# A pre-activation block with look-up convolutions: its products in four column tiles of 128 rows and 32 columns

## The chip, the cores and the metric

The kernel runs on one core of one Trainium2 chip. A core has five engines with a queue each: TensorE (PE in the profile, its weight loads PEld), VectorE (DVE), ScalarE (ACT), GpSimd (POOL) and SyncE (SP, which here only issues DMAs). TensorE writes to PSUM, which VectorE and ScalarE read. The metric is the device time of one execution in microseconds; lower is better. The kernel before took 2607.75 us in the median of three runs (2605.92 to 2608.51).

## The reference

The input is 16 images of 256 channels with 28 x 28 points, fp32. It is normalised over groups of 8 channels, passed through two "look-up" convolutions with batch norm between and after them, gated by a squeeze-and-excite layer, and added to the input.

```python
def amm_conv3x3(x, centroids, w_sub):              # centroids (256, 16, 9), w_sub (256, 9, 256)
    p = the 3x3 patches of each channel            # (b, n, c, 9), n = 28*28
    d = sum(p*p) - 2*einsum('bncs,cks->bnck', p, centroids) + sum(centroids*centroids)
    attn = softmax(-d, axis=-1)                    # over 16 centroids
    lut = einsum('cks,cso->cko', centroids, w_sub)
    return einsum('bnck,cko->bno', attn, lut)

x0 = groupnorm(x)
out = relu(bn1(amm_conv3x3(x0, centroids1, wsub1)))
out = bn2(amm_conv3x3(out, centroids2, wsub2))
out = out * sigmoid(relu(mean(out) @ w1 + b1) @ w2 + b2)
result = x + relu(out + x0)
```

So for each channel and point there is a softmax over 16 distances, the mean of the 16 centroids under it (9 numbers), and then a product of these 256 x 9 numbers with `w_sub` to 256 output channels. That last product is the one the change touches.

## The kernel before

**Blocks.** The work of a layer and an image is cut in four blocks: half of the input channels (`hh`, 128 of them) times half of the rows (`t`, 14 rows of 28 points, N = 392 columns). 2 layers x 16 images x 4 make 128 blocks. For each of them TensorE runs:

- `logits` (line 613, tile name `lg`): four calls of 16 matmuls with 32 rows and 32 columns of weights, one for each of the 16 places (4 row groups, 4 column groups) of the array. ScalarE turns the result into exponentials `e` (line 624).
- `num_b` (line 678, `nb`): the denominators and the ninth of the weighted means, 32 matmuls of 64 rows and 32 columns that accumulate over four steps.
- `num_a` (line 664, `na`): the other eight means, four calls of eight matmuls of 64 rows and 32 columns.

VectorE takes the reciprocals and spreads them over partitions, VectorE and GpSimd scale the means, and nine operands `q` of 128 x 392 are ready for each block (tiles `qp`, two in each, and `qo`).

**Products.** `product` (lines 744 to 751, tile `acc`) multiplies nine `q` by nine weight matrices of 128 x 128 and accumulates in one PSUM bank. The 2 x 2 blocks of channels and rows are combined with sums of weights and differences of `q` (made by `mix` on GpSimd, line 757), so that seven products are enough where eight would be needed; one of the seven is issued in two parts, of seven matmuls and of two. That is eight calls of `product` for each layer and image, listed in `PRODUCTS` (lines 45 to 48). ScalarE (line 779) and VectorE (lines 785 and 787) take the results out of PSUM. The very last product is cut in two halves of 196 columns.

**Small matmuls.** Beside products stand `gn_mean` and `gn_var` (lines 534 and 551, `gnp`: group means and variances of the next image, 128 x 128 weights `gmat`, 2 to 4 columns), `center_add` (line 343, `sqp`), `rest_sum` (line 1146, once at the end), `se_hidden` (line 1041, `sep`: 128 rows, 32 columns of weights, 1 column of data) and `se_gate` (line 1049, 32 rows and 128 columns).

**Order.** The order of every engine's queue is written by hand. `at(cl, sub, f, ...)` files a call under a step and a place within it, and in the end all calls are issued in the order of these keys; each engine then works through its own in that order, and semaphores hold an instruction back until its operands are there. Between two products stand calls of `lg`, `na` or `nb`, so that TensorE changes between forms of tiles all the time. PSUM is used as four pairs of banks, handed out by the tables `ROLES` and `EARLY`.

**How fp32 shows.** Each fp32 matmul of the program stands in the trace as two weight loads and two matmuls ("passes"), so a product of nine is 18 rows of LDWEIGHTS and 18 of MATMUL.

Of the kernel before, what the change touches and what calls it, by code (L numbers as in the profile page):

```python
# [17 lines left out]
P = 128  # L18
# [59 lines left out]


BIAS_ROW = 11  # L80


def rows_of(m, c, a):
# [5 lines left out]
def kernel(  # L89
# [22 lines left out]
    nc = tc.nc  # L112
# [9 lines left out]
    one = const.tile([P, 1], F32, name="one")  # L122
# [3 lines left out]
    gmat = const.tile([P, P], F32, name="gmat")  # L126
# [18 lines left out]
    def bank(name, step=None, role=None, tag=None):  # L145
        return banks(name, step, role, tag)[:, 0, :]
# [4 lines left out]
    def view(t, off, dims):  # L151
        return bass.AP(t.tensor, t.offset + off, [list(d) for d in dims])
# [25 lines left out]
    def spare_of(n0, n, i=0):  # L178
        return pts[i].rearrange("p s n -> p (s n)")[:, n0 : n0 + n]
# [14 lines left out]
    def load(ap, name, eng=None):  # L194
        t = const.tile(list(ap.shape), ap.dtype, name=name)
        (eng or nc.sync).dma_start(t, ap)
        return t
# [18 lines left out]
    wl = {n: walls[i // 3][:, i % 3] for i, n in enumerate(("S1", "S2", "S4", "A12", "S3", "A22"))}  # L216
# [37 lines left out]
    first = io.tile([P, 1568], F32, tag="pb", name="first")  # L254
# [25 lines left out]
    nhalf_sb = load(nhalf, "nhalf_sb")  # L280
# [28 lines left out]
    def rsqrt(dst, src, eps, n):  # L309
        t = small.tile([P, n], F32, name="rs_t")  # L310
        nc.gpsimd.tensor_scalar(t, src, eps, None, op0=ALU.add)
        nc.gpsimd.tensor_tensor(dst, t, mhalf[:, :n], ALU.pow)
# [20 lines left out]
    def small_bank(name, step, tag=None):  # L333
        return bank(name, step, step and ROLES["small"][step % 2], EARLY["small"].get(step) if tag is None else tag)
# [5 lines left out]

    def center_add(wf, c0, w, sq, step=None):
        ps = small_bank("sqp", step)
        nc.tensor.matmul(ps[:, :w], lhsT=nhalf_sb, rhs=sq[:, :w], start=True, stop=True)  # L343
        nc.vector.tensor_add(wf[:, c0 : c0 + w], wf[:, c0 : c0 + w], ps[:, :w])

    def center_sum(wf, n):
# [162 lines left out]
    def border(u, p):  # L509
# [18 lines left out]
        ends = row[:, :, 0 : W : W - 1]  # L528
        eng.tensor_tensor(ends, ends, view(tm, 16 * (4 + 2 * t) + 8 * p, [tm.ap[0], [1, 8], [16, 2]]), ALU.add)

    def gn_mean(b, k0=0, n=NB, step=None):
        st, mv = gst[b]
        ps = small_bank("gnp", step)[:, : 2 * n]
        nc.tensor.matmul(  # L534
            ps, lhsT=gmat, rhs=mv[:, k0 : k0 + n].rearrange("p b t -> p (b t)"), start=True, stop=True
        )
        gm = small.tile([P, NB, 2], F32, name="gn_gm")
        nc.vector.tensor_copy(gm[:, :n].rearrange("p b t -> p (b t)"), ps)
        dv = small.tile([P, NB], F32, name="gn_dv")
        nc.vector.tensor_sub(dv[:, :n], ps.rearrange("p (b t) -> p b t", t=2)[:, :, 0], mv[:, k0 : k0 + n, 0])  # L540
        for i in range(n):
            nc.vector.scalar_tensor_tensor(
                dv[:, i : i + 1], ps[:, 2 * i : 2 * i + 1], mv[:, k0 + i, 0:1], dv[:, i : i + 1],
                op0=ALU.subtract, op1=ALU.mult,
            )
        gst[b, "m"] = gm, dv

    def gn_var(b, k0=0, n=NB, step=None):
        gm, dv = gst.pop((b, "m"))
        ps = small_bank("gnp", step)[:, :n]  # L550
        nc.tensor.matmul(ps, lhsT=gmat, rhs=dv[:, :n], start=True, stop=True)  # L551
        var = small.tile([P, NB], F32, name="gn_var")
        rstd, shift = (nrm[:, b, i, k0 : k0 + n] for i in (1, 2))
        if n == 1:
            neg = small.tile([P, NB], F32, name="gn_neg")
            nc.vector.tensor_scalar_mul(neg[:, :n], gm[:, :n, 0], -1.0)
            nc.vector.scalar_tensor_tensor(var[:, :n], ps, GN_EPS, gm[:, :n, 1], op0=ALU.add, op1=ALU.add)
            nc.gpsimd.tensor_tensor(rstd, var[:, :n], mhalf[:, :n], ALU.pow)
            nc.gpsimd.tensor_tensor(shift, neg[:, :n], rstd, ALU.mult)
        else:  # L560
            nc.vector.tensor_add(var[:, :n], gm[:, :n, 1], ps)
            rsqrt(rstd, var[:, :n], GN_EPS, n)
            nc.gpsimd.tensor_tensor(shift, gm[:, :n, 0], rstd, ALU.mult)
            nc.gpsimd.tensor_scalar(shift, shift, -1.0, None, op0=ALU.mult)
# [177 lines left out]
    accs = {}  # L742

    def product(key, us, w, ks, first=True, last=True, step=None, cols=(0, N), tag=None):
        if first and key not in accs:
            accs[key] = bank("acc", step, step and ROLES["acc"][step % 2], EARLY["acc"].get(step) if tag is None else tag)
        for n, k in enumerate(ks):
            nc.tensor.matmul(  # L748
                accs[key][:, : cols[1] - cols[0]], lhsT=wl[w][:, k, :], rhs=us["q", k][:, cols[0] : cols[1]],
                start=first and n == 0, stop=last and n == len(ks) - 1,  # L750
            )

    def mix(out_u, mm, in0, in1):
        if mm == 4:
# [356 lines left out]
    vsum = spare_of(NB * S * P + 2 * N, NB * P, 1).rearrange("p (o n) -> p o n", o=NB)  # L1111
# [31 lines left out]
    def rest_sum(b, tag):  # L1143
        ps = bank("pv", tag=tag)[:, :NB]
        for o in range(NB):
            nc.tensor.matmul(ps[:, o : o + 1], lhsT=vsum[:, o, :], rhs=one, start=True, stop=True)
        ys[b, "rest"] = rest[:, 1]
        nc.vector.tensor_tensor(rest[:, 1], ps, rest[:, 0], ALU.mult)

# [86 lines left out]
    for j, u in enumerate(blocks):  # L1236
        gi, g = 8 * (j // 4), 2 * j
        for mm in range(5):
            kind = "one" if mm == 4 else "pair"
            t = g + 1 + (j > 2) if mm == 4 else g + 2 + (j > 1)  # L1240
# [59 lines left out]
    for l in range(2):  # L1300
        for b in range(B):
            n = l * B + b
            g = 8 * n
            us = blocks[4 * n : 4 * n + 4]
            for c, w, r, ks in PRODUCTS:
                if g + c == 5:
                    for sub, k0, k1 in ((0.8, 0, 5), (0.82, 5, 7), (0.84, 7, 9)):
                        at(4, sub, product, (n, c), us[r], w, ks[k0:k1], k0 == 0, k1 == 9, step=4)
                elif n == 2 * B - 1 and c == 11:
                    for sub, k0, k1 in ((1.95, 0, 5), (1.97, 5, 7), (1.99, 7, 9)):  # L1310
                        at(g + c, sub, product, (n, c), us[r], w, ks[k0:k1], k0 == 0, k1 == 9, tag=0)
                elif n == 2 * B - 1 and c in (9, 10):
                    at(g + c, 2.0, product, (n, c), us[r], w, ks, tag=c - 9)
                elif n == 2 * B - 1 and c == 12:
                    at(g + c, 1.99, open_last, n)
                    for h in range(2):
                        at(g + c, 2.0 + 0.02 * h, product, (n, 12 + h), us[r], w, ks, cols=(N // 2 * h, N // 2 * h + N // 2))
                else:
                    at(g + c, 1.32 if g + c == 7 else 2.0, product, (n, c), us[r], w, ks, step=g + c)
# [15 lines left out]
            if n == 2 * B - 1:  # L1335
# [13 lines left out]
                at(g + 11, 1.9, norm_out, l, b, *c12)  # L1349
                at(g + 11, 1.91, norm_out, l, b, *c22)  # L1350
                at(g + 11, 1.96, rest_sum, b, 1)
                at(g + 11, 1.98, se_hidden, b, None, 1)
                at(g + 11, 1.995, se_gate, b, None, 1)
# [23 lines left out]
            if l == 0:  # L1377
# [8 lines left out]
                if b + 1 < B:  # L1386
                    at(*(((8, 1.6) if b == 1 else (g - 2, 2.6)) if b else (1, 1.6)), load_x, b + 1)
                    for q in range(NB):
                        at(*(((g + 1, 1.5) if b == 1 else (g, 0.3)) if b else (4, 0.14)), gn_stats, b + 1, q)
                    at(*((g + 1, 2.1) if b else (4, 0.825)), gn_mean, b + 1, step=g + 1 if b else 4)  # L1390
                    at(*((g + 3, 2.1) if b else (4, 0.845)), gn_var, b + 1, step=g + 3 if b else 4)
                    for q in range(NB):
                        at(*((g + 4, 1.9) if b else (4, (0.95, 1.055)[q])), gn_apply, b + 1, q)
                        at(*((g + 4, 1.92) if b else (4 + 4 * q, 1.6 - 0.05 * q)), to_home1, b + 1, q)
            else:
                last = b == B - 1
# [93 lines left out]
    ps = bank("gnq", tag=3)  # L1490
# [59 lines left out]
    with tc.If(rv > 0):  # L1550
        with tc.For_i(0, B, 1) as it:
            t = io.tile([P, NB, HW], F32, tag="xt", name="xt")
# [6 lines left out]
            for k in range(NB):  # L1559
                gn_stats(B, k)  # L1560
            gn_mean(B)
            gn_var(B)
            for k in range(NB):
                gn_apply(B, k)
                nc.gpsimd.dma_start(home1[B][k * P : (k + 1) * P], twice(xpads[k]))
            for l in range(2):
# [6 lines left out]
                for t2 in range(2):  # L1573
                    us = []
# [51 lines left out]
def _lay_out(inputs):  # L1626
# [52 lines left out]
    for p in range(P):  # L1679
# [3 lines left out]
        for b in range(2):  # L1683
            before[p, b, : b * P + p] = 1.0
        nhalf[p, p - p % 16 + BIAS_ROW] = -0.5 if p % 16 in rows else 0.0
        if p % 16 == BIAS_ROW:
            a = (p // 16) % 2
# [37 lines left out]
```

## Time and profile before

| | |
|---|---|
| time, median of three runs | 2607.75 us (2605.92 to 2608.51) |
| the profiled execution, first to last instruction | 2606.2 us |
| TensorE busy, matmuls | 2591.2 us, 99%, 37026 instructions |
| TensorE busy, weight loads | 1273.2 us, 49% |
| VectorE, ScalarE, GpSimd busy | 1776.6, 1371.7, 1905.6 us |
| products, line 748, all groups, busy | 1097.5 + 182.4 + 157.9 us and a small group |
| `lg`, `na`, `nb`, busy | 469.0, 376.5, 375.2 us |

The profile is of one execution. Its span is what lies between its first and its last instruction; the timed runs include a little around it. A group of instructions is given as "line, engine, operation, out<-in, rows*columns of the weights, partitions x elements of the data, count". Busy time of a group is the time in which at least one of its instructions ran, while "mean ns" is the length of a single one; where matmuls overlap, as in a pipeline or in several tiles, the mean is longer than busy time over count. So 15872 `lg` passes of 499 ns are busy for only 469.0 us.

In the timeline, instructions of one kind that follow each other are merged in one row: its start, the time to the end of the last, and the count.

### The profile page before, as it was taken

Reading aid. Unit: us, or ns where it says so; the run is one execution under the profiler, and the core shown is the slowest. Engines: PE = TensorE matmul, PEld = TensorE weight load, DVE = VectorE, ACT = ScalarE, POOL = GpSimd, SP = SyncE. Lnnn points to the kernel's source line nnn. Section 1 sums busy time; section 2 is a strip of 40 time slices with the busy share of each in tenths; the row PEclk is TensorE's granted clock in tenths of the full one; section 3 lists DMA queues with packets and bytes.
Section 4 is the critical chain, followed back from the end, with each engine's and each line's share of the span. In section 5 each row is a group of like instructions: output and inputs, shape, how many; then the busy total and the mean of one; then the engine's idle time right before and its main releaser. Section 6 shows DMA issues by size and latency. Waiting matters only on the chain.

```text
span 2606.2 us, 85832 instructions
## 1 busy us (share of the span) xinstructions
PE 2591.2 (99%) x37026; PEld 1273.2 (49%) x37026; DVE 1776.6 (68%) x3797; ACT 1371.7 (53%) x1913; POOL 1905.6 (73%) x1341
## 2 busy tenths in 40 slices
PE   8999999999999999999999999999999999999999
PEld 4444455444454444544444444444444444444445
DVE  8766656666657666566676767766776667767676
ACT  6444444444444445444445555555555655555565
POOL 6687666776567776667666887878878787787786
PEclk9999999999999999999999999999999999999999
DMA  7556656565545575564664444444344444444442
GB/s 228 166 131 184 195 166 187 160 168 170 163 141 147 157 194 173 165 172 134 176 169 103 109 112 127 119 119 120 101 126 128 118 116 112 115 124 128 117 104 66
DMA packets 213288, 372.07 MB, mean 143 GB/s; under 512 B 29496, under 2 KB 183528, under 8 KB 212328
## 3 DMA queue, kind: packets, MB, share of 16 engines
q1 hardware_dynamic: 206584, 333.75, 47.6%
q0 software_dynamic: 6176, 32.66, 3.5%
q8 instruction: 295, 4.83, 0.8%
q14 instruction: 89, 0.73, 0.1%
q10 hardware_dynamic: 144, 0.10, 0.0%
HBM read 288.46 MB, written 77.95 MB: 141 GB/s over the span
## 4 chain that ended last, share of the span: by engine, by line
PE 99%; ACT 0%; POOL 0%; DVE 0%; issue 0%; DMA 0%; POOLq 0%; ACTq 0%
PE acc L748 52%; PE lg L613 17%; PE na L664 14%; PE nb L678 14%; ACT e L624 0%; PE sep L1049 0%; POOL qp L757 0%; PE sep L1041 0%; DMA xt<-in_x 0%; PE tap L392 0%; PE sqp L374 0%; PE sqp L343 0%; POOL qp L729 0%; PE gnp L534 0%; PE gnp L551 0%
## 5 line engine op out<-in xcount | busy, mean ns | idle before, releaser
L748 PE MATMUL acc<-qp,wall 128*128 128x392 f32 (+1 forms) x3088 | 1097.5, 498 | 0.3 <-POOL qp L757 0.2
L624 ACT ACTIVATE e<-lg 128x784 f32<-128x784 f32 x960 | 737.8, 820 | 635.2 <-PE lg L613 632.0
L757 POOL TENSOR_TENSOR qp<-qp,qp 128x784 f32<-128x784 f32 x512 | 943.7, 1867 | 152.0 <-DVE qp L740 151.6
L748 PEld LDWEIGHTS acc<-qp,wall 128*128 128x128 f32 x3088 | 567.4, 190 | 504.8 <-issue 53.6
L721 DVE STREAM_SHUFFLE rb<-r 128x392 f32<-128x392 f32 x1024 | 551.5, 606 | 0.0
L613 PE MATMUL lg<-pt,wd 32*32 32x392 f32 x15872 | 469.0, 499 | 0.2
L692 DVE SCALAR_TENSOR_TENSOR r<-nb,kst,r 128x392 f32<-128x392 f32 x128 | 80.1, 626 | 447.6 <-ACT r L688 447.6
L664 PE MATMUL na<-e,cwa 64*32 64x392 f32 x8192 | 376.5, 493 | 0.0
L740 DVE TENSOR_TENSOR qp<-na,rb 128x784 f32<-128x784 f32 x352 | 334.0, 972 | 62.2 <-PE na L664 50.3
L678 PE MATMUL nb<-e,cwb 64*32 64x392 f32 x8192 | 375.2, 492 | 0.1
L729 POOL TENSOR_TENSOR qo<-qo,rb 128x392 f32<-128x392 f32 x128 | 132.5, 1035 | 297.0 <-DVE rb L717 296.2
L706 DVE RECIPROCAL r<-r 128x392 f32<-128x392 f32 x128 | 333.2, 2603 | 4.4
L729 POOL TENSOR_TENSOR qp<-qp,rb 128x784 f32<-128x784 f32 x160 | 295.7, 1858 | 2.9
L678 PEld LDWEIGHTS nb<-e,cwb 64*32 64x32 f32 x8192 | 191.5, 106 | 174.7 <-issue 24.5
L664 PEld LDWEIGHTS na<-e,cwa 64*32 64x32 f32 x8192 | 183.8, 106 | 184.0 <-issue 74.8
L613 PEld LDWEIGHTS lg<-pt,wd 32*32 32x32 f32 x15872 | 116.4, 103 | 266.6 <-issue 238.3
L748 PE MATMUL acc<-qp,w_A 128*128 128x392 f32 x512 | 182.4, 499 | 0.0
L688 ACT ACTIVATE r<-nb,kst 128x392 f32<-128x392 f32 x128 | 86.7, 678 | 165.5 <-PE nb L678 162.3
L648 POOL TENSOR_TENSOR z<-z,mx 128x1568 f32<-128x1568 f32 x32 | 91.8, 2869 | 94.8 <-DVE mx L642 94.8
L748 PE MATMUL acc<-qo,wall 128*128 128x392 f32 (+1 forms) x386 | 157.9, 491 | 0.0
L734 ACT COPY qp<-na 128x784 f32<-128x784 f32 x160 | 130.0, 813 | 23.6 <-PE na L664 22.1
L748 PEld LDWEIGHTS acc<-qp,w_A 128*128 128x128 f32 x512 | 94.6, 190 | 82.5 <-DVE qp L740 19.8
(241 smaller groups left out, 1706.4 us busy)
## 6 DMA issues: line engine op xcount, KB each, us to landing
pt<-home SPq DMA_DIRECT2D x744, 209.0 KB
pt<-home SPq DMA_DIRECT2D x744, 104.5 KB
home<-xpad SPq DMA_DIRECT2D x30, 899.0 KB
xt<-in_x SPq DMA_DIRECT2D x30, 784.0 KB
out_dram<-y SPq DMA_DIRECT2D x31, 392.0 KB
pt<-in_p SPq DMA_DIRECT2D x6, 784.0 KB
d_wS<-st SPq DMA_DIRECT2D x12, 192.0 KB
wall<-d_wS SPq DMA_DIRECT2D x4, 576.0 KB
```

The lines of the kernel that those rows point to most:

```text
L613: nc.tensor.matmul(bk[32 * c : 32 * c + 32, :N].rearrange("p (r w) -> p r w", w=W), lhsT=(wx[u["hh"]] if early(u) else wts["wd", u["hh"]]) ...
L624: nc.scalar.activation(eg[:, 2 * i : 2 * i + 2, :], bk[:, :, :N], AF.Exp, scale=2.0)
L648: nc.gpsimd.tensor_tensor(zk, zk, mx.unsqueeze(2).to_broadcast([P, N // 4, K]), ALU.subtract)
L664: nc.tensor.matmul(bs[32 * i : 32 * i + 32, r, :N], lhsT=wts["cwa", u["hh"]][64 * r : 64 * r + 64, mm, i, :], rhs=es[64 * r : 64 * r + 64, ...
L678: nc.tensor.matmul(bs[32 * i : 32 * i + 32, r, :N], lhsT=wts["cwb", u["hh"]][64 * r : 64 * r + 64, mm, i, :], rhs=es[64 * r : 64 * r + 64, ...
L706: nc.vector.reciprocal(u["r"], u["r"])
L721: nc.vector.stream_shuffle(rb[:, r, :], u["r"], mask_of(2 * mm + r))
L729: nc.gpsimd.tensor_tensor(q, q, u.pop(("rb", mm)), ALU.mult)
L734: nc.scalar.copy(pair(u, mm), u.pop(("na", mm))[:, :, :N])
L740: nc.vector.tensor_mul(pair(u, mm), u.pop(("na", mm))[:, :, :N], rb)
L748: nc.tensor.matmul(accs[key][:, : cols[1] - cols[0]], lhsT=wl[w][:, k, :], rhs=us["q", k][:, cols[0] : cols[1]], start=first and n == 0, s ...
L757: nc.gpsimd.tensor_tensor(pair(out_u, mm), pair(in0, mm), pair(in1, mm), ALU.subtract)
```

## The change

`product` issues four matmuls for each of its nine operands in place of one. Each takes 32 of the 128 columns of the weights (`wl[w][:, k, o:o+32]`), all 128 rows and the same 392 columns of `q`, and writes 32 of the 128 partitions of the same PSUM bank. `start` and `stop` are set for each of the four as before. A helper `by_cols` does the same for the small matmuls of `center_add`, `gn_mean`, `gn_var` and `rest_sum`; `se_hidden` and `se_gate` are as they were. Nothing else differs: other engines have the same instructions in the same order, and lines after 548 move down by some (`product`'s matmul from 748 to 752, `lg` from 613 to 616, `na` from 664 to 667, `nb` from 678 to 681, `sep` from 1041 to 1045 and from 1049 to 1053; `gnp` is issued in `by_cols` at line 534).

```diff
+AW = 32
...
     def center_add(wf, c0, w, sq, step=None):
         ps = small_bank("sqp", step)
-        nc.tensor.matmul(ps[:, :w], lhsT=nhalf_sb, rhs=sq[:, :w], start=True, stop=True)
+        by_cols(ps[:, :w], nhalf_sb, sq[:, :w])
...
+    def by_cols(ps, lhsT, rhs):
+        for o in range(0, P, AW):
+            nc.tensor.matmul(ps[o : o + AW], lhsT=lhsT[:, o : o + AW], rhs=rhs, start=True, stop=True)
+
     def gn_mean(b, k0=0, n=NB, step=None):
...
-        nc.tensor.matmul(
-            ps, lhsT=gmat, rhs=mv[:, k0 : k0 + n].rearrange("p b t -> p (b t)"), start=True, stop=True
-        )
+        by_cols(ps, gmat, mv[:, k0 : k0 + n].rearrange("p b t -> p (b t)"))
...
     def gn_var(b, k0=0, n=NB, step=None):
...
-        nc.tensor.matmul(ps, lhsT=gmat, rhs=dv[:, :n], start=True, stop=True)
+        by_cols(ps, gmat, dv[:, :n])
...
         for n, k in enumerate(ks):
-            nc.tensor.matmul(
-                accs[key][:, : cols[1] - cols[0]], lhsT=wl[w][:, k, :], rhs=us["q", k][:, cols[0] : cols[1]],
-                start=first and n == 0, stop=last and n == len(ks) - 1,
-            )
+            for o in range(0, P, AW):
+                nc.tensor.matmul(
+                    accs[key][o : o + AW, : cols[1] - cols[0]], lhsT=wl[w][:, k, o : o + AW],
+                    rhs=us["q", k][:, cols[0] : cols[1]], start=first and n == 0, stop=last and n == len(ks) - 1,
+                )
...
     def rest_sum(b, tag):
         ps = bank("pv", tag=tag)[:, :NB]
         for o in range(NB):
-            nc.tensor.matmul(ps[:, o : o + 1], lhsT=vsum[:, o, :], rhs=one, start=True, stop=True)
+            by_cols(ps[:, o : o + 1], vsum[:, o, :], one)
```

## The prediction

> **What bounds the kernel now.** I read the page first (span, engine shares, chain), then who TensorE waits for, then the timeline of TensorE alone.
>
> ```profile
> span 2606.2 us, 85832 instructions
> ...
> PE 2591.2 (99%) x37026; PEld 1273.2 (49%) x37026; DVE 1776.6 (68%) x3797; ACT 1371.7 (53%) x1913; POOL 1905.6 (73%) x1341
> ...
> PEclk9999999999999999999999999999999999999999
> ...
> PE 99%; ACT 0%; POOL 0%; DVE 0%; issue 0%; DMA 0%; POOLq 0%; ACTq 0%
> ```
>
> ```profile
> PE gnp L436 <- DVE gn_mv L425: 5.6, 1, 5.6
> PE flp L1219 <- DVE fl L1215: 0.7, 1, 0.7
> ```
>
> TensorE is busy from one end to the other at its full clock, and the list of its waits begins with one wait of 5.6 us at the start and goes on with fractions of a microsecond. So the span is the sum of what stands in TensorE's own queue, and every nanosecond of a block there counts as often as the block occurs. The other engines have a quarter of the span or more to spare.
>
> ```profile
> 1003.53 4.22 PE L748 MATMUL acc<-qp,wall 128*128 128x392 f32 x12
> 1007.59 0.82 PE L748 MATMUL acc<-qo,wall 128*128 128x392 f32 x2
> 1008.24 1.48 PE L748 MATMUL acc<-qp,wall 128*128 128x392 f32 x4
> 1009.65 0.94 PE L613 MATMUL lg<-pt,wd 32*32 32x392 f32 x32
> 1010.52 2.92 PE L664 MATMUL na<-e,cwa 64*32 64x392 f32 x64
> 1013.38 0.94 PE L613 MATMUL lg<-pt,wd 32*32 32x392 f32 x32
> ...
> 1034.36 1.58 PE L748 MATMUL acc<-qp,wall 128*128 128x392 f32 x4
> 1035.87 1.50 PE L613 MATMUL lg<-pt,wd 32*32 32x392 f32 x26
> ```
>
> Read the start times. Each fp32 matmul of the program appears as two passes, so a product of nine is 18 passes. It lasts from 1003.53 to 1009.65, 6.12 us; the two-matmul product of four passes lasts 1.51 us. The difference, 4.61 over 14 passes, is 0.3293 us a pass, and 6.12 - 18 x 0.3293 = 0.193 us is a fixed price of each product block. The tiled blocks around it have the same round: lg is 16 tiles in two rounds and lasts 0.87 us, so its fixed price is 0.211; na is eight tiles in eight rounds, 2.86 us, fixed 0.226 (starts are shown to 0.01 us). The array therefore streams no faster in tiles than in one piece: sixteen 32-row tiles, eight 64-row tiles or one full tile take one 0.329 us round each. The change leaves the number of rounds as it is, and can only move the fixed prices.
>
> **The fixed price of a block, taken apart.**
>
> ```profile
> L748 PE MATMUL acc<-qp,wall x3088: 329/492/597, 58.1 to 2600.5; 128*128 128x392 f32 x191, 128*128 128x196 f32 x2
> L748 PE MATMUL acc<-qp,w_A x512: 492/492/597, 41.2 to 2545.0; 128*128 128x392 f32 x171
> L748 PE MATMUL acc<-qo,wall x386: 329/492/493, 62.2 to 2599.9; 128*128 128x392 f32 x191, 128*128 128x196 f32 x2
> L748 PE MATMUL acc<-qo,w_A x64: 492/492/493, 45.2 to 2543.7; 128*128 128x392 f32 x64
> L613 PE MATMUL lg<-pt,wd x15872: 484/487/513, 69.0 to 2559.2; 32*32 32x392 f32 x199
> L664 PE MATMUL na<-e,cwa x8: 511/511/513, 424.1 to 424.2; 64*32 64x392 f32 x8
> 255.11 0.61 PE L613 MATMUL lg<-pt,wd 32*32 32x392 f32 x16
> 424.09 0.62 PE L664 MATMUL na<-e,cwa 64*32 64x392 f32 x8
> L1041 PEld LDWEIGHTS sep<-ysum,w_sb x68: 106/112/113, 1430.3 to 2591.6; 128*32 128x32 f32 x68
> L1041 PE MATMUL sep<-ysum,w_sb x68: 170/170/191, 1430.3 to 2591.6; 128*32 128x1 f32 x68
> ```
>
> The rows "x n: a/b/c" give minimum, median and maximum duration in ns. (a) First pass: 597 against 492 for a product, 105 ns, because the first weight load of 128 columns has nothing to hide under; 513 against 487 for lg, 26 ns. sep is the one line that already runs the new form, 128 rows by 32 columns: 191 against 170, 21 ns. (b) Stagger: the 16 first passes of lg cover 0.61 us, though one lasts 0.513, so the last tile starts 0.10 after the first; na's eight cover 0.62, so 0.107. A tile keeps its lag to the end of its block. A product in one piece has none. (c) The rest, about 0.09 us in all three (0.193 - 0.105 = 0.088; 0.211 - 0.026 - 0.10 = 0.085; 0.226 - 0.024 - 0.107 = 0.095), is the array running empty before another tile form starts; it stays.
>
> **Term 1, the product blocks.** There are eight products for each of 16 images and two layers, 256, and each stands between lg or na/nb blocks (a handful at the very end do not). Per layer and image they are 126 passes; 32 x 126 = 4032, and 18 more for the last product, which is cut in two halves: 4050, as the rows have it (3088 + 512 + 386 + 64). Gain in (a): 105 - 21 = 84 ns, 256 times, 21.5 us. Loss in (b): the unknown stagger S of four tiles of 128 rows. No row shows it, so bounds:
> - lg's pace, 0.10 us over 15 gaps, 6.7 ns a tile: S = 20 ns.
> - na's mean pace, 0.107 over 7: 15 ns a tile, S = 46.
> - na's first four tiles, whose rows are half of a new tile's:
>
> ```profile
> 424.09:424.12 0.03, 0.03 (x3) 1.00 0.86 171
> 424.09:424.14 0.05, 0.05 (x4) 1.00 0.60 136
> 1751.55 0.20 PEld L1041 LDWEIGHTS sep<-ysum,w_sb 128*32 128x32 f32 x4 [0.56 <-issue]
> ```
>
> The number in brackets counts the passes that had started: the fourth starts between 0.03 and 0.05 us after the first. With twice the rows, 58 to 98, middle 78.
> - sep's four loads, in one tile, cover 0.20 us at 0.113 each: (0.20 - 0.113)/3 = 29 ns a load. With one load for each later tile S = 87; with both passes' loads of each tile in line ahead of the next, 3 x 58 = 174.
> - Both tiled forms fill the whole array in 0.10 us whatever the number of tiles: S = 100.
>
> I take 80 ns: between 78 and 87, the two that carry 128 rows. Term 1 is 256 x (80 - 84) = -1.0 us, with ends 256 x (20 - 84) = -16.4 and 256 x (174 - 84) = +23.0. So the saved load wait and the new stagger nearly cancel, and the result hangs on S.
>
> [...]
>
> **Term 2, the small matmuls beside products.**
>
> ```profile
> 1750.80 0.82 PE L748 MATMUL acc<-qo,wall 128*128 128x392 f32 x2
> 1751.56 0.29 PE L1041 MATMUL sep<-ysum,w_sb 128*32 128x1 f32 x4
> 1751.77 0.94 PE L613 MATMUL lg<-pt,wd 32*32 32x392 f32 x32
> 410.98 1.48 PE L748 MATMUL acc<-qp,wall 128*128 128x392 f32 x4
> 412.29 0.28 PE L534 MATMUL gnp<-gn_mv,gmat 128*128 128x4 f32 x2
> 412.50 0.94 PE L613 MATMUL lg<-pt,wd 32*32 32x392 f32 x32
> ```
>
> sep (L1041) is a form of its own now: the array empties before it and it costs 0.21 us more (1751.56 to 1751.77). Afterwards it has the product's form and sits in column tile 0 alone, which is S ahead of the last tile. It starts 0.329 after that tile's last pass and ends some 0.02 us behind the others' end: 0.19 saved, 16 times, -3.0 us (0.13 saved, -2.1, if S is 20).
>
> gnp (L534 and L551) has the product's form now and keeps it, in four pieces. It follows the last pass without a gap (410.98 + 4 x 0.329 = 412.30) and costs 0.21 less the 0.09 that the product would have paid anyway, 0.12. In pieces each tile has two passes some 30 ns apart (sep's pace) and no load of 128 columns: 0.03 + 0.10 - 0.09 = 0.04. Saved 0.08, 30 times, -2.4 us. The other end, eight loads of 29 ns in line, is 0.23 + 0.07 - 0.21 = 0.09 dearer, +2.7. center_add (six passes) and rest_sum (four) are below 0.5 us together. se_gate's row form (32 x 128) stays alone as before.
>
> **Terms at nothing.** Passes of products grow from 4050 to 16200 with as many loads. A product would issue 72 in 6.1 us, one in 85 ns; lg issues 32 in 0.87, one in 27. The loads hide under the running round, as na's do. Waits: the tiled program waits in the same places, on the first of each four. acc is ready up to S later for ScalarE and VectorE, which wait for it off the path; were that cover gone, it would be 256 x 0.08 = 20 us. Queues other than TensorE's have the same instructions in the same order, so no DMA moves past another.
>
> **Sum.** -1.0 - 3.0 - 2.4 = -6.4 us on the profile's 2606.2. The median of the runs is 1.55 above that span; 2607.75 - 6.4 = 2601.35, say 2601.4, 0.25% faster. With S between 60 and 95: 256 x (60 - 84) - 5.4 = -11.5 to 256 x (95 - 84) - 5.4 = -2.6, 2596 to 2605.
>
> **Rivals.** Two runs of this kernel tell 0.2%, 5.2 us, from no change; that is S below 85 for faster and above 125 for slower.
> - *Short stagger* (S 20 to 60): the four tiles start at lg's pace because loads of different column tiles do not hinder each other. For it: sixteen tiles start within 0.10 us. Against: the pace fell from 6.7 to 15 ns as rows doubled. 256 x (20 - 84) - 5.4 = -21.8 to -11.5: 2586 to 2596.
> - *The wait moves* (S 95 to 125): the array's first fill costs 0.10 us in any tiling, and the 0.084 saved is spent on it. For it: lg and na agree on 0.10 with 16 and 8 tiles. Against: four loads fewer than na's eight. -2.6 to +5.1: 2605 to 2613.
> - *Loads in line* (S 125 to 174), the slower side: in the first round both passes' weights of one tile load before the next tile's. Place: the head of each of the 256 blocks; price 58 ns a tile; it decides from S = 125 on. For it: sep's four loads stand 29 ns apart. Against: those are in one tile, and lg's tiles overlap theirs. +5.1 to +17.6: 2613 to 2625.
> - *Longer rounds*: a pass in four tiles takes longer than 0.3293, since a load with 128 rows meets matmuls on all rows or the four tiles fetch the same data. Each nanosecond is 4050 x 0.001 = 4.05 us; from 2.6 ns on it makes the kernel slower, and a whole exposed wait of 21 to 29 ns gives 4050 x 0.021 - 6.4 = +79 to +111, 2686 to 2719. Against: na's round with both row halves in use is 0.329 too. [...]
>
> ```profile
> L748 PEld LDWEIGHTS acc<-qp,wall 128*128 128x128 f32 x3088 | 567.4, 190 | 504.8 <-issue 53.6 <-POOL qp L757 21.3 <-DVE qp L740 20.4
> ```
>
> **How the numbers follow.** Forecast 0.37 (0.27 of it beyond 0.2% faster, 0.10 within), short stagger 0.22, the wait moves 0.13, loads in line 0.18, longer rounds 0.10. Faster 0.27 + 0.22 = 0.49; same 0.10 + 0.13 = 0.23; slower 0.18 + 0.10 = 0.28. The likeliest gives 2601.4, its own range is 2596 to 2605. The range runs from 2585, just below S = 20, to 2618, S = 146: out stay the upper half of loads in line and most of longer rounds, under 0.2.
>
> **What would show it.** In the changed profile: 16200 product passes of form 128*32; a product of nine from its first pass to the next block's first, 6.12 us before, 6.116 if S is 80 (6.06 for 20, 6.21 for 174); the first round's four passes spread by S; first passes some 21 ns longer than the others, not 105; rounds still 0.329; sep no longer adding 0.21 between a product and lg; gnp to lg 0.13 instead of 0.21. Wrong would be the whole reading if TensorE showed new waits, or if rounds changed.

## The result and the profile after

| | before | changed |
|---|---|---|
| time, median (range, runs) | 2606.02 us (2603.88 to 2610.24, 12) | 2599.61 us (2597.72 to 2603.99, 12) |
| profiled execution, its span | 2606.2 us | 2598.2 us (its time 2599.72) |
| ratio | | 0.9975, 95% interval 0.9967 to 0.9984 |

The time is the one forecast, 6.4 us less. It comes about in another way, though: the products gained far more than the forecast gave them, and `lg`, which the change doesn't touch, took 15.5 us more. First the page of the changed kernel.

```profile
span 2598.2 us, 110542 instructions
...
PE 2580.0 (99%) x49386; PEld 1043.7 (40%) x49386; DVE 1783.5 (69%) x3797; ACT 1373.1 (53%) x1913; POOL 1916.9 (74%) x1341
...
L752 PE MATMUL acc<-qp,wall 128*32 128x392 f32 x12352 | 1090.6, 492 | 0.7 <-POOL qp L761 0.3
...
L616 PE MATMUL lg<-pt,wd 32*32 32x392 f32 x15872 | 481.8, 499 | 1.9 <-issue 1.9
...
L667 PE MATMUL na<-e,cwa 64*32 64x392 f32 x8192 | 373.9, 493 | 0.0
...
L681 PE MATMUL nb<-e,cwb 64*32 64x392 f32 x8192 | 371.8, 492 | 0.2 <-ACT e L627 0.2
```

TensorE is still busy 99% of the span. Its products are shorter, and `lg` is busy for 481.8 us where it was 469.0, with 1.9 us of idle time put down to "issue", in which it waited for nothing that the profile shows. Now the timeline of TensorE, at the product that the prediction took apart before, then the same passes through three windows of 10, 20 and 30 ns (width, busy time with the count of passes that had started, granted clock, and two columns on DMA), and the row with minimum, median and maximum of a pass in ns.

```profile
1004.29 4.16 PE L752 MATMUL acc<-qp,wall 128*32 128x392 f32 x48
1008.27 0.84 PE L752 MATMUL acc<-qo,wall 128*32 128x392 f32 x8
1008.93 1.50 PE L752 MATMUL acc<-qp,wall 128*32 128x392 f32 x16
1010.36 0.96 PE L616 MATMUL lg<-pt,wd 32*32 32x392 f32 x32
1011.24 2.90 PE L667 MATMUL na<-e,cwa 64*32 64x392 f32 x64
1014.08 0.96 PE L616 MATMUL lg<-pt,wd 32*32 32x392 f32 x32
```

```profile
1004.29:1004.30 0.01, 0.01 (x1) 1.00 0.00 0
1004.29:1004.31 0.02, 0.01 (x3) 1.00 0.00 0
1004.29:1004.32 0.03, 0.03 (x4) 1.00 0.00 0
```

```profile
L752 PE MATMUL acc<-qp,wall x12352: 326/492/518, 58.1 to 2592.5; 128*32 128x392 f32 x198, 128*32 128x196 f32 x2
```

The product lasts from 1004.29 to 1010.36, 6.07 us against 6.12. Its four first passes have all started within 30 ns (at 0, 7, 13 and 20 ns in the trace): the stagger S is 20 here, not 80. First passes last at most 518 ns against 492. In layer 1 nearly all products start so; in layer 2 the four start at 0, 7, 22 and 38 ns. In the median a product of nine lasts 6.062 us in layer 1 and 6.078 in layer 2, against 6.122.

The small matmuls, `gnp` at one place and `sep` at another, with the rows of before that the prediction does not show:

```profile
407.20 4.16 PE L752 MATMUL acc<-qp,wall 128*32 128x392 f32 x48
...
413.15 0.22 PE L534 MATMUL gnp<-gn_mv,gmat 128*32 128x4 f32 x8
413.30 1.01 PE L616 MATMUL lg<-pt,wd 32*32 32x392 f32 x32
```

```profile
1743.88 4.17 PE L752 MATMUL acc<-qp,wall 128*32 128x392 f32 x48
1747.86 0.86 PE L752 MATMUL acc<-qo,wall 128*32 128x392 f32 x8
1748.51 0.26 PE L1045 MATMUL sep<-ysum,w_sb 128*32 128x1 f32 x4
1748.70 0.94 PE L616 MATMUL lg<-pt,wd 32*32 32x392 f32 x32
```

```profile
406.26 4.22 PE L748 MATMUL acc<-qp,wall 128*128 128x392 f32 x12
```

```profile
1746.75 4.22 PE L748 MATMUL acc<-qp,wall 128*128 128x392 f32 x12
```

Product and `gnp` together take 413.30 - 407.20 = 6.10 us, before 412.50 - 406.26 = 6.24. Product and `sep` take 1748.70 - 1743.88 = 4.82, before 1751.77 - 1746.75 = 5.02.

**Where the time went.** I cut TensorE's time at the first pass of every block, so that each block has all time up to the next one's start, and summed by kind; what stands ahead of the first block, and the last block, are left out, some 17 us of each span. The last two columns are two later executions of the same kernel, which the experiments below bring.

| us | before | changed | changed, a2 | changed, a3 |
|---|---|---|---|---|
| products | 1370.3 | 1354.6 | 1355.7 | 1354.6 |
| `lg` | 455.5 | 471.0 | 465.7 | 462.4 |
| `na` and `nb` | 734.1 | 728.0 | 728.6 | 728.5 |
| the rest | 29.0 | 27.3 | 27.5 | 27.4 |
| span | 2606.2 | 2598.2 | 2594.8 | 2590.0 |
| layer 1, `lg` blocks late by over 0.1 us: count, sum | 4, 1.9 | 15, 11.8 | 5, 5.7 | 5, 3.2 |
| layer 1, other `lg` blocks, lateness in all | 0.6 | 5.9 | 6.3 | 6.3 |

Products and the rest gained 15.7 + 1.7 = 17.4 us, and 16.1 and 17.3 in the two later executions. `lg` lost 15.5 in two parts (lateness is a block's time over 0.870 us, the shortest). About 6 us are a small lateness, 16 to some 80 ns a block, there in each execution. Most of it comes back in the blocks behind: in layer 1 a block of `na` is 16 ns shorter and one of `nb` 31 in the mean, 3 us together, and products win 2 more, as e1 and e8 show below. The other 3 us of the 6.1 that `na` and `nb` gained are seven stalls that they had in the profile of before. The other part of what `lg` lost are stalls, and these come and go: 11.8 us here, 3.2 in a3. One of them, in the changed kernel's timeline, and what TensorE waited for between 280 and 1100 us:

```profile
353.99 0.88 PE L616 MATMUL lg<-pt,wd 32*32 32x392 f32 x14
355.15 0.98 PE L616 MATMUL lg<-pt,wd 32*32 32x392 f32 x18 [0.27 <-issue]
```

```profile
PE lg L616 <- issue: 1.9, 7, 0.5
PE sqp L534 <- ACT e L627: 0.3, 1, 0.3
```

An `lg` block of 32 passes breaks off after 14 and goes on 1.16 us after its start, and the profile shows no other engine that holds it.

### The profile page after: what moved, and what is told of

It is laid out like the page before. It is cut to its first block, busy times and chain, and to the rows that moved or that the text cites. A ratio compares the mean times of both kernels' runs of the same rounds, so it can differ in the third digit from the quotient of the medians.

```text
span 2598.2 us, 110542 instructions
## 1 busy us (share of the span) xinstructions
PE 2580.0 (99%) x49386; PEld 1043.7 (40%) x49386; DVE 1783.5 (69%) x3797; ACT 1373.1 (53%) x1913; POOL 1916.9 (74%) x1341
## 4 chain that ended last, share of the span: by engine, by line
PE 98%; ACT 1%; DVE 1%; POOL 0%; issue 0%; DMA 0%; POOLq 0%; ACTq 0%
PE acc L752 52%; PE lg L616 18%; PE na L667 14%; PE nb L681 14%; ACT e L627 0%; ACT pt L1139 0%; PE sep L1053 0%; POOL qp L761 0%; DMA xt<-in_x 0%; PE tap L393 0%; PE sqp L375 0%; PE sqp L534 0%; DVE qp L743 0%; POOL qp L732 0%; PE gnp L534 0%
## 5 line engine op out<-in xcount | busy, mean ns | idle before, releaser
L752 PE MATMUL acc<-qp,wall 128*32 128x392 f32 x12352 | 1090.6, 492 | 0.7 <-POOL qp L761 0.3
L752 PEld LDWEIGHTS acc<-qp,wall 128*32 128x32 f32 x12352 | 403.8, 110 | 639.4 <-issue 539.8
L724 DVE STREAM_SHUFFLE rb<-r 128x392 f32<-128x392 f32 x1024 | 558.9, 613 | 0.0
L616 PE MATMUL lg<-pt,wd 32*32 32x392 f32 x15872 | 481.8, 499 | 1.9 <-issue 1.9
L667 PEld LDWEIGHTS na<-e,cwa 64*32 64x32 f32 x8192 | 176.9, 106 | 188.6 <-issue 75.2
L681 PEld LDWEIGHTS nb<-e,cwb 64*32 64x32 f32 x8192 | 177.3, 106 | 185.7 <-issue 45.9
L616 PEld LDWEIGHTS lg<-pt,wd 32*32 32x32 f32 x15872 | 123.8, 103 | 289.0 <-issue 237.9
L752 PE MATMUL acc<-qp,w_A 128*32 128x392 f32 x2048 | 181.6, 494 | 0.0
L752 PE MATMUL acc<-qo,wall 128*32 128x392 f32 x1544 | 163.5, 491 | 0.0
L759 POOL TENSOR_TENSOR qo<-qo,qo 128x392 f32<-128x392 f32 x128 | 132.3, 1034 | 0.1
```

The costliest lines, as they stand in the source:

```text
L616: nc.tensor.matmul(bk[32 * c : 32 * c + 32, :N].rearrange("p (r w) -> p r w", w=W), lhsT=(wx[u["hh"]] if early(u) else wts["wd", u["hh"]]) ...
L667: nc.tensor.matmul(bs[32 * i : 32 * i + 32, r, :N], lhsT=wts["cwa", u["hh"]][64 * r : 64 * r + 64, mm, i, :], rhs=es[64 * r : 64 * r + 64, ...
L681: nc.tensor.matmul(bs[32 * i : 32 * i + 32, r, :N], lhsT=wts["cwb", u["hh"]][64 * r : 64 * r + 64, mm, i, :], rhs=es[64 * r : 64 * r + 64, ...
L724: nc.vector.stream_shuffle(rb[:, r, :], u["r"], mask_of(2 * mm + r))
L752: nc.tensor.matmul(accs[key][o : o + AW, : cols[1] - cols[0]], lhsT=wl[w][:, k, o : o + AW], rhs=us["q", k][:, cols[0] : cols[1]], start=f ...
L759: nc.gpsimd.tensor_tensor(out_u["q", 8], in0["q", 8], in1["q", 8], ALU.subtract)
```

## The experiments

Each ratio is against the kernel before in the same session. e1 to e4 ran on one chip, a2, e5, e8 and e9 on another at a later time, and the last four together.

**What belongs to the small matmuls, and what to each layer (e1, e2, e3).** e1 leaves the small matmuls whole:

```diff
-        for o in range(0, P, AW):
-            nc.tensor.matmul(ps[o : o + AW], lhsT=lhsT[:, o : o + AW], rhs=rhs, start=True, stop=True)
+        nc.tensor.matmul(ps, lhsT=lhsT, rhs=rhs, start=True, stop=True)
```

> Products in four tiles as in the change, the small matmuls of the group means, center_add and rest_sum whole again. Theory: a whole small matmul beside a tiled product is a form of its own, so each of the 30 group-mean matmuls pays an emptied array on both sides and a first load of 128 columns, about 0.3 us where the change pays 0.02 (5.949 + 0.150 - 6.078 by its blocks): 30 x 0.29 = 8.7 us more than the change, about 2608, no faster than before (ratio 1.000 to 1.002). Rival: these small matmuls do not matter, the ratio stays that of the change, 0.9975.

Measured: 2599.91 us (2597.46 to 2602.55), ratio 0.998, interval 0.9971 to 0.9989. Its timeline:

```profile
405.09 4.17 PE L751 MATMUL acc<-qp,wall 128*32 128x392 f32 x48
...
411.17 0.39 PE L533 MATMUL gnp<-gn_mv,gmat 128*128 128x4 f32 x2
411.49 0.94 PE L615 MATMUL lg<-pt,wd 32*32 32x392 f32 x32
```

The time missed the theory, but the place did what it said: product and whole `gnp` take 6.40 us, 0.30 more than in four pieces, 30 times, 9 us. What the theory could not know is that its base, the 2599.6 of the changed kernel, held stalls: e1 has 1.4 us of them in `lg` of layer 1, and one pause of 1.85 us in a product. Against a3, which took 2591.4 in a later session with few stalls, e1 is 8.5 us longer by the medians and 7.3 by the ratios, near the 9. e1 shows one more thing: with `gnp` whole, a product of nine of layer 1 lasts 6.078 us, as in layer 2, and its four tiles start at 0, 7, 22 and 38 ns. So 16 of the 60 ns that layer 1's products gained come with `gnp` in four pieces, and so does `lg`'s small lateness.

e2 splits only layer 2's products and leaves the small ones whole; e3 splits only layer 1's, and the small ones.

```diff
+        aw = (128, 32)[us["l"]]
...
-            for o in range(0, P, AW):
+            for o in range(0, P, aw):
```

> Only the products of layer 2 in four tiles, all else as before the change (rest_sum too). Theory: the gain of the change comes from layer 2 alone, because layer 1 gives its own back in the lg blocks: by the two profiles layer 2's blocks went from 1317.9 to 1310.4 us, layer 1's from 1271.2 to 1270.5. So about -7.5 us, ratio 0.997. Rival: the two layers share the gain evenly and the longer lg blocks belong to that one profile: -3.2 us, ratio 0.9988.

Measured: 2597.67 (2597.0 to 2598.61), ratio 0.9971, interval 0.996 to 0.9982. This is the theory's number: 128 blocks of 44 ns are 5.6 us, and `sep` gave 16 times 0.156, 2.5 us.

> Only the products of layer 1 in four tiles, with the small matmuls in tiles as in the change. Theory: products gain about 8 us and small ones 2, and lg blocks lose about 15 while na and nb win 6 back: -0.7 us, ratio 0.9997, and the profile shows layer 1's lg blocks near 247 us against 233 before. Rival (even shares): -3.2 us, ratio 0.9988, lg unchanged.

Measured: 2598.58 (2597.42 to 2608.76), ratio 0.9979, interval 0.997 to 0.9987. The median gained 6.6 us, more than theory and rival said. The blocks say 128 x 0.060 = 7.7 us for the products and 30 x 0.08 = 2.4 for `gnp`. In the profiled execution, which took 2608.76 and so was slower than before, `lg` lost 8.2 us in stalls and 6.2 in lateness, the theory's 15. Two of 12 executions lay near 2608. So what the theory said of `lg` holds in the profiled execution and does not fit the median, which was the first sign that the loss in `lg` is not a fixed price.

**How many tiles (e4), and in which order (e5).** e4 has two column tiles in place of four:

```diff
-AW = 32
+AW = 64
```

> Two tiles of 64 columns in place of four of 32, products and small matmuls. Theory for a block: the first wait grows with the columns, 21 ns at 32 and 105 at 128, so 49 at 64; one gap of 7 to 16 ns as stagger; a product of nine 6.073 to 6.082 us, 256 times 40 to 49 ns = -10 to -12.5; sep stays a form of its own (no -3), group means about -2. If what lg loses goes with the number of TensorE instructions (8100 product passes in place of 16200 added to nothing), it loses a third to a half of 9 us net: total -8 to -10, ratio 0.9965; with no such loss -13, ratio 0.995. Rival: lg loses because products are tiled at all, not because of their number: -4 us, ratio 0.9985.

Measured: 2591.93 (2590.88 to 2593.86), ratio 0.9951, interval 0.9938 to 0.9964, the case without a loss in `lg`. A product of nine lasts 6.076 us, as expected, and the page gives `lg` back what the changed kernel's took:

```profile
L752 PE MATMUL acc<-qp,wall 128*64 128x392 f32 x6176 | 1088.1, 494 | 0.4 <-POOL qp L761 0.3
...
L616 PE MATMUL lg<-pt,wd 32*32 32x392 f32 x15872 | 468.0, 499 | 0.0
```

e5 keeps the four tiles and issues three operands for one tile before the next tile's:

```diff
-        for n, k in enumerate(ks):
-            for o in range(0, P, AW):
...
+        for k0 in range(0, len(ks), 3):
+            for o in range(0, P, AW):
+                for n, k in list(enumerate(ks))[k0 : k0 + 3]:
```

> The products' order of issue: for each group of three operands the first column tile's matmuls, then the second's and so on, so six passes and not two stand between the starts of two neighbouring tiles. Theory: the stagger of the tiles is set by how many instructions stand ahead of a tile in the queue, 7 ns a tile where the queue is full and 16.6 where it is not, for two passes; with six it is 20 to 50 ns a tile, 60 to 150 for the block, against 20 to 38 now: +40 to +110 ns in 256 blocks, +10 to +28 us, 2610 to 2628. Rival: the stagger comes from the first weight load of each tile alone and a tile's later passes wait for their own tile, not in the queue: no change, 2599 to 2602. A third way: the first tile runs ahead with its six passes before the others have any, then a tile starts only when the six before it have been issued, and a block grows by up to three rounds, 0.99 us in 256 blocks, up to +250 us.

Measured: 3361.21 (3360.73 to 3364.18), ratio 1.2906, interval 1.2888 to 1.2923. The third way came nearest and was three times too small: 756 us, 256 times 2.95. Timeline and windows of the seven-matmul product at 1205.94:

```profile
1205.94 5.99 PE L753 MATMUL acc<-qp,wall 128*32 128x392 f32 x44
...
1213.51 0.94 PE L616 MATMUL lg<-pt,wd 32*32 32x392 f32 x32
```

```profile
1205.94:1206.62 0.68, 0.68 (x3) 1.00 0.00 0
1205.94:1206.64 0.70, 0.70 (x4) 1.00 0.00 0
1205.94:1207.32 1.38, 1.38 (x9) 1.00 0.37 151
```

It takes 7.57 us where seven matmuls took 4.75. In the first 0.68 us only three passes have started. In a product of nine of the same profile the first tile's passes start at 0, 355 and 684 ns, and the second tile's first at 690, with no pass of that tile ahead of it. The first tile's other three follow at 1013, 1342 and 1671. The third tile starts at 1378, 6 ns after the second matmul of the tile before it, as the second tile did. Why the tiles start so late no run shows. In the change, which issues one operand for all four tiles in turn, all four have started within 20 to 38 ns.

**Whether the loss in `lg` belongs to the program (a2, a3), and which part of it (e8, e9).** a2 is the changed kernel without an edit.

> The changed kernel once more, without an edit, for a second profile of the 15 us that its lg blocks of layer 1 took more than before (247.4 against 232.6 us busy), while e3, which has the same matmuls in layer 1, took 2598.6 in the median and 2608.8 in the execution that was profiled. Theory: the lost time belongs to the program and comes in every execution: about 2599.6, ratio 0.9975, lg of layer 1 between 244 and 250 us in the profile. Rival: it comes and goes from one execution to the next: times in two groups, near 2586 without and near 2600 with it, and lg either at 232 or at 247.

Measured: 2592.26 (2591.23 to 2596.37), ratio 0.9951, interval 0.9938 to 0.9965. The theory falls, and neither group of the rival was met: the median moved by 7 us from one session, and perhaps one chip, to another. The profiled execution (2596.37, the slowest of the five) has its `lg` loss mostly in one place. Windows of it, columns as before: busy time of each engine, granted clock, DMA share, GB/s.

```profile
944.00:947.00 3.00, 3.00 (x82) 1.33 (x67) 2.63 (x7) 2.35 (x3) 0.71 (x1) 1.00 0.94 290
947.00:950.00 3.00, 0.93 (x30) 0.23 (x30) 2.85 (x8) 0.82 (x1) 3.00 (x3) 1.00 0.68 206
950.00:954.00 4.00, 4.00 (x45) 0.99 (x60) 0.08 (x1) 0.82 (x1) 4.00 (x3) 0.57 0.35 96
```

```profile
949.95 1.06 PE L616 MATMUL lg<-pt,wd 32*32 32x392 f32 x13 [2.07 <-issue]
```

TensorE stood for 2.07 us, and from 950 to 954 us the granted clock was 0.57.

e8 has the small matmuls in two pieces among products in four; e9 has the products whole and the small ones in four.

```diff
-        for o in range(0, P, AW):
-            nc.tensor.matmul(ps[o : o + AW], lhsT=lhsT[:, o : o + AW], rhs=rhs, start=True, stop=True)
+        for o in range(0, P, 2 * AW):
+            nc.tensor.matmul(ps[o : o + 2 * AW], lhsT=lhsT[:, o : o + 2 * AW], rhs=rhs, start=True, stop=True)
```

```diff
-            for o in range(0, P, AW):
+            for o in range(0, P, P):
...
-                    accs[key][o : o + AW, : cols[1] - cols[0]], lhsT=wl[w][:, k, o : o + AW],
+                    accs[key][o : o + P, : cols[1] - cols[0]], lhsT=wl[w][:, k, o : o + P],
```

> Products in four pieces of 32 columns, the small matmuls of by_cols (gnp, sqp, rest_sum) in two pieces of 64 columns. Theory: the loss in lg is set off by the small matmuls in four pieces among products in four pieces, since e1, with the small ones whole, lost nothing there (lg 232.1 us in layer 1) and e4 neither (231.8): lg 232 us, and the time is that of the changed kernel less its loss, 2599.6 - 15, with some 0.1 us for each of 30 changes of form between a product and gnp, +3 to +5: 2587 to 2590, ratio 0.993 to 0.994. Rival: the loss comes from four times the instructions in the products whatever stands beside them: lg 244 to 250 us, 2599 to 2605.

Measured: 2597.36 (2595.58 to 2599.29), ratio 0.9968, interval 0.9956 to 0.998. In `lg` it is as the theory said, in the time it is not, again because 2599.6 was no base. Beside a2 of the same session it is 5.1 us longer, and its timeline has them:

```profile
404.88 4.17 PE L752 MATMUL acc<-qp,wall 128*32 128x392 f32 x48
...
410.95 0.29 PE L534 MATMUL gnp<-gn_mv,gmat 128*64 128x4 f32 x4
411.17 0.94 PE L616 MATMUL lg<-pt,wd 32*32 32x392 f32 x32
```

Product and `gnp` take 6.29 us against 6.10; 30 x 0.19 = 5.7. The small lateness of `lg` is gone in e8 (0.7 us in layer 1) as in e1 (0.6), while the changed kernel, a2, a3 and e3 have 5.9 to 6.4. Its products of layer 1 last 6.078 us, as in e1.

> The other half alone: products whole as before, the small matmuls of by_cols in four pieces of 32 columns. Theory as for e8 (four-piece small matmuls set off the loss, whatever the products are): lg of layer 1 at 240 us or more, and 2606 + 8 to + 18, 2614 to 2624. Rival (the products' instructions are needed for it): lg 232 us, and only the change of form beside gnp is paid, +0.1 us for each of 30, 2606 to 2612.

Measured: 2606.87 (2605.58 to 2612.13), ratio 1.0008, interval 0.9999 to 1.0017: the rival's. The lateness is 1.5 us. So most of the steady part came here with both, products and small matmuls in four pieces; layer 2, where no `gnp` runs, has 0.2 us of it in the changed kernel's profile and 0.3 before. Stalls are another matter: e9, with whole products, has an `lg` block in which TensorE stood for 1.96 us, between 1302.5 and 1305.2 us, and a granted clock of 0.55 from there to 1309, so a single large one came without split products.

**Versions beside each other (a3, e4 again, e6, e7).** All on one chip, before 2604.61 (2603.53 to 2606.82).

> The changed kernel a third time, on one chip with e4b, e6 and e7. Theory, from the 2592.3 of the second time and its profile (stalls of 5.7 us in lg blocks of layer 1 against 11.8 in the first profile): the stalls are no fixed price of the program but come and go with the execution and with the session; the median lies anywhere from 2590 to 2601. Rival: 2592.3 was the exception, the median is 2599 to 2601 again.

Measured: 2591.43 (2589.3 to 2595.63), ratio 0.9952, interval 0.9939 to 0.9966, in the theory's range. The group of `lg` in its profile, and its wait in the same stretch from 280 to 1100 us, where "issue" no longer stands:

```profile
L616 PE MATMUL lg<-pt,wd 32*32 32x392 f32 x15872 | 475.6, 499 | 0.1
```

```profile
PE sqp L534 <- ACT e L627: 0.3, 1, 0.3
```

> AW = 64 again, beside the changed kernel on the same chip. Theory: two column tiles have half as many instructions as four and keep the queue filled; there are no such stalls (1.1 us in the first profile), so the time is steady, 2591 to 2593. Against AW = 32 without stalls the blocks themselves are 13 ns longer, 256 x 0.013 = 3.3 us, so where a3 comes out near 2590 the two are equal within 2 us, and where a3 comes out near 2600, e4 is 8 us faster. Rival: the first 2591.9 was luck of the session, 2597 or more.

Measured: 2591.1 (2589.76 to 2592.85), ratio 0.9949, interval 0.9935 to 0.9962: steady, and equal to a3.

e6 gives `sep` the form of two tiles as well (a third zeroed block of weights, so that 64 columns can be taken from `k` on):

```diff
-            nc.tensor.matmul(ps, lhsT=w1_sb[:, k, :], rhs=term, start=n == 0, stop=n == len(terms) - 1)
+            nc.tensor.matmul(ps, lhsT=w1_sb[:, k : k + 2, :].rearrange("p a b -> p (a b)"), rhs=term, start=n == 0, stop=n == len(terms) - 1)
...
-        nc.scalar.activation(hid, ps, AF.Relu, bias=b1_sb, scale=1.0 / HW)
+        nc.scalar.activation(hid, ps[: 2 * RED], AF.Relu, bias=b1_sb, scale=1.0 / HW)
```

> AW = 64, and sep gets the products' form too: its weights are taken 64 columns wide (32 of them beside what is needed, with zeros or with the other half's weights), its result 64 partitions of which ScalarE reads the first 32 as before. Theory: sep follows the product without the array running empty in between, as it does in the changed kernel, where the product and sep together took 4.632 + 0.192 = 4.824 against 4.759 + 0.216 = 4.975 with AW = 64: 0.11 to 0.15 us saved 16 times, -1.8 to -2.4 us, 2589 to 2590, ratio 0.9940. Rival: sep's place is covered or the wider load eats it: equal to e4.

Measured: 2591.57 (2590.33 to 2592.75), ratio 0.9949, interval 0.9935 to 0.9963: the rival's, no gain.

```profile
1734.32 4.17 PE L753 MATMUL acc<-qp,wall 128*64 128x392 f32 x24
...
1738.97 0.34 PE L1046 MATMUL sep<-ysum,w_sb 128*64 128x1 f32 x4
1739.25 0.94 PE L617 MATMUL lg<-pt,wd 32*32 32x392 f32 x32
```

Product and `sep` take 4.93 us; with AW = 64 and the old `sep` they took 4.975, with four tiles 4.82. `sep` starts 0.10 us sooner behind the product, but its loads of 64 columns take 138 ns in place of 113, and `sep` lasts 0.27 in place of 0.216. What is left, 0.044 us 16 times, is 0.7.

e7 takes 64 columns in layer 1 and for the small matmuls, 32 in layer 2:

```diff
+        aw = (64, 32)[us["l"]]
```

> The products of layer 1 and the small matmuls in two pieces of 64 columns, the products of layer 2 in four of 32, where sep has the same form. Theory: layer 2 gains what a block of four tiles is shorter than one of two, 128 x 0.013 = 1.7 us, and sep's 16 x 0.14 = 2.2 us, and keeps lg free of stalls, since those of the changed kernel stood in layer 1 (11.8 of 11.9 us): 2587 to 2589, ratio 0.9933 to 0.994. Rival: the instructions of layer 2 bring stalls of their own or stalls in layer 1 by way of the later queue: 2593 or more.

Measured: 2590.3 (2589.28 to 2591.76), ratio 0.9947, interval 0.9933 to 0.996. Layer 2 has `sep`'s gain (4.82 us again), but a product of nine there lasts 6.079 us, no less than one of two tiles (6.076), so the 1.7 us are missing. e7, e4, e6 and a3 lie within 1.3 us with ranges that overlap; these runs do not tell them apart.

## Why the prediction came out

The number was right by luck: two wrong terms of about the same size stand behind it in that session.

- **TensorE bounds, rounds stay.** Right. TensorE is 99% busy before and after, behind the wait at the start none on another engine is above 1.1 us, and rounds take 0.329 us; the longer rounds are out.
- **(a) The first load's wait, 105 ns to 21.** Right: first passes last at most 518 against 492, 26 ns in place of 21.
- **(b) The stagger S, taken as 80.** This is the step that failed. It is 20 to 23 ns in most of layer 1 and 38 in layer 2 (and 38 in layer 1 too where `gnp` is not in four pieces). Both numbers that I leaned on, twice `na`'s pace (78) and `sep`'s loads in line (87), did not hold for the product's four tiles; the low bound, `lg`'s pace of 6.7 ns a tile (S = 20), is met in most of layer 1. A block is 60 ns shorter in layer 1 and 44 in layer 2, so term 1 is 128 x 0.060 + 128 x 0.044 = 13.3 us and not 1.0. The rival "short stagger" named this, and its 2586 to 2596 holds the medians of both later sessions.
- **(c) The 0.09 us before another form.** Right: the trace has 0.42 us from the last pass of a product to `lg`'s first, before and after, 0.09 over a round, and neither a load nor a pass starts in between.
- **Term 2.** Right. `gnp` with its product gained 6.24 - 6.10 = 0.14, less the 0.060 that are term 1's: 0.08, 30 times 2.4 us, as forecast. `sep` gained 0.20 - 0.044, 16 times 2.5 us, between the 3.0 taken and the 2.1 given for S = 20. That these forms matter is shown from the other side by e1 (9 us by the places with `gnp` whole) and e8 (5.7 us with it in two pieces).
- **Terms at nothing.** Not all right. No engine waited anew, but `lg` did not stay: by 6 us of lateness that the blocks behind it return for the most part, and by stalls, 10 us more than before in the first session.

The sum by blocks, -13.3 - 4.9 = -18.2 (-17.4 by the table), is 11 to 12 us beyond the forecast; the stalls of that session gave back most of this. Where they were few, the same kernel ran at ratios of 0.9951 and 0.9952.

**The stalls.** They are shown to be no fixed price: three profiles of one program have 11.8, 5.7 and 3.2 us of them. The kernel has 110542 instructions against 85832, and the pages of before and of the changed kernel list a DMA queue of the kind "instruction" (packets, MB, share of the DMA engines):

```profile
q8 instruction: 295, 4.83, 0.8%
q8 instruction: 392, 6.42, 1.1%
```

A packet is 16.4 KB, and in both traces there is one for 255 instructions of TensorE (75172 and 99879 with its queue's own). I counted TensorE's instructions from its first, and looked at all pauses of more than 0.36 us between two starts within a block, at full clock and without a semaphore to wait for, from 60 to 2540 us in all 14 profiles. There are 28. In 22 of them, the longest among them, the places of the first instruction after the pause are a multiple of 256 apart (the 30146th before, the 17858th, 30402nd and 40386th in the changed kernel), and it starts 1.39 to 1.64 us after such a packet has landed. One instruction, the 30402nd, is late in three profiles (changed, a3, e3). What holds TensorE in these pauses is not shown: no run changed how the packets come.

**What stays open.** The other six pauses stand elsewhere: one in before, and five, in blocks late by 6.0 us together, in the first profile of the changed kernel, the one shown above among them. What these are, and why times were longer in all 12 executions of the first session (only one was profiled), the runs do not say. The three sessions of the experiments were on three chips, so session and chip cannot be told apart. How `gnp` in four pieces brings `lg`'s small lateness and the shorter stagger beside it is open too.

## What to carry to other kernels

Where a kernel changes between forms of tiles all the time, look at the fixed price of each change, which is 0.2 us here. Two things made the 17 us: a first weight load of 32 columns in place of 128 (a first pass of 518 ns in place of 597, 79 less, at 20 to 38 ns of stagger, 256 times), and small matmuls in the form of the product beside them (0.08 and 0.16 us, 46 times). Splitting a full matmul in four column tiles cost 20 to 38 ns of stagger a product here with one operand issued for all tiles in turn; issuing three for one tile first made the kernel 29% slower (e5). Two tiles gave as much as four here (2591.10 against 2591.43 us) with half the instructions in the products. Before building on a difference of 0.3%, take the same kernel in a second session.

## What was not expected of the hardware

- In most of layer 1 a column tile of 128 rows starts 6 to 9 ns after the one before it, close to the 6.7 ns of `lg`'s tiles of 32 rows; in most of layer 2 the gaps are 7, 15 and 16 or 17 ns.
- In e5 a column tile without a pass of its own took its first one only 6 ns after its neighbour's second matmul had started (690 ns against 684), and the kernel took 756 us more than before.
- 22 of 28 pauses of TensorE end 1.39 to 1.64 us after a packet of the queue "instruction" has landed, all at places a multiple of 256 instructions apart.
- After TensorE had stood for 2.07 us (a2) and 1.96 us (e9) the granted clock was 0.57 and 0.55 in the windows behind it (4.0 and 3.8 us); e1 has a pause of 1.85 us, and its granted clock is 1.000 in the mean of the whole profile.
